# Weighting v three neighbours at a time in row groups of TensorE, with the last convolution group moved from ScalarE taps to TensorE

## The chip, the cores and the metric

The kernel runs on one core of one Trainium2 chip. The metric is the device time of one execution in microseconds (us); the median of several executions is given. A profile of one execution shows what each engine did: PE is TensorE (matmul) and PEld its weight loads, DVE is VectorE, ACT is ScalarE, POOL is GpSimd, and SP issues most of the DMAs.

## The reference

Two layers on `x` of shape (16, 56, 56, 384), float32. Each normalises its input in 32 groups of 12 channels (per image), applies an operation and adds the result to its input.

```
# layer 0: dilated attention; 3 dilations (1, 2, 3) of 128 channels each, 4 heads of 32 channels per dilation
qkv  = w_qkv @ groupnorm(x)
attn[n, k] = softmax_k( sum_d q[n, d] * k[neighbour k of n, d] * 32**-0.5 )    # 9 neighbours, zeros outside
y[n, d]    = sum_k attn[n, k] * v[neighbour k of n, d]
x = x + w_proj @ y + b_proj
# layer 1: depthwise 3x3 convolution, weights sign(w), zeros outside
x = x + conv3x3_depthwise(groupnorm(x), sign(clip(w, -1, 1)))
```

## The kernel before, in words

Channels lie on the 128 partitions, in three groups of 128 (`NG = 3`; group g has dilation g+1 in layer 0). Pixels are cut into chunks of 8 rows, 448 pixels (`PX`), 7 chunks per image and 112 in all (`N`). Three plans write each chunk's work into a table of steps: `plan_a` turns x to channel-major and takes the statistics of layer 0, `plan_b` does the attention, `plan_c` the convolution. Each chunk begins 9 steps (`STEP`) after the one before it; `plan_a` runs 9 chunks ahead of `plan_b`, `plan_c` 10 chunks behind. `at(when, order, piece)` notes a piece; the pieces are then emitted in order of step and, within a step, in the order SOFTMAX, SCORE, CONVOLVE, WEIGH, QUERY, QKV, PROJECT, STAGE_A, STAGE_C, NORM, LOADS. The Tile framework sets the final order on each in-order engine queue and inserts the waits; `in_one_go` keeps the matmuls of a burst together.

The pieces of a chunk that the change and the prediction touch:

- `project` (L357): k, v and q by float32 matmuls of 448 columns. `k_or_v` copies to persistent tiles with halo rows; two or three slots of them exist.
- `score` (L408) multiplies q by three shifted copies of k at once on VectorE (tile `t` of 3 x 448); `score_round` (L392) sums over the 32 channels of a head with a 0/1 matrix of 32 columns, four neighbours at once into the four column groups of TensorE.
- `softmax_1` (L418 to 429) turns the scores to pixel-major with `perm`, and VectorE takes the maximum and the difference; `softmax_2` divides by the sum; `softmax_3` (L443 to 446) splits each float32 weight into three bf16 terms; `turn_weights` (L451) turns them back, one group at a time (108 rows: 3 terms x 4 heads x 9 neighbours).
- `weigh` (L464, 467, 474), 27 times a chunk, three per step: one bf16 matmul copies one neighbour's 4 weights to the 32 channels of each head and adds the three terms (K = 108 rows, 128 columns out, PSUM tile `pb_a`, two banks in turn); VectorE multiplies by the shifted v into `w`; GpSimd adds `w` to `y`, 8 adds for each group.
- `out_project` (L488 to 494): projection, bias and residual, statistics of layer 1.
- Convolution of channel groups 0 and 1 (`JG = 2`): `load` brings three row-shifted copies of 32 channels onto 96 partitions (3 DMAs), `normalise` (L558) is 4 ScalarE instructions, `convolve` (L575) is 12 float32 matmuls of 32 columns in the four column groups, and VectorE adds the residual (L582).
- Convolution of group 2: `load_g` (1 DMA), `normalise_g` (L600), `taps_g` (L609: 9 ScalarE products with the tap's weight; L615: 2 GpSimd adds of three maps at once), `sum_g` (L620, 623: 3 GpSimd adds of one map).
- `turn` (L630) transposes the result to pixel-major; ScalarE copies it out of PSUM (L632); SP stores it.

`ps_mt` is a pool of four PSUM banks for all other matmul results; `ps_q` and `ps_s` have one bank each, `ps_bc` two: eight in all. A float32 matmul appears in the profile as two PE instructions.

Of the kernel before, what the change touches and what calls it, by code (L numbers as in the profile page):

```python
# [8 lines left out]
F32 = mybir.dt.float32  # L9
BF16 = mybir.dt.bfloat16  # L10
AF = mybir.ActivationFunctionType
ALU = mybir.AluOpType
# [14 lines left out]
NR = NG * HEADS * NTAP  # L27
K_SLOTS, V_SLOTS = 2, 3
# [4 lines left out]
def dilated_attention_then_binary_conv(  # L33
# [27 lines left out]

# [9 lines left out]
    JG = NG - 1  # L71
# [5 lines left out]
    ps_mt = ctx.enter_context(tc.tile_pool(name="ps_mt", bufs=4, space=PSUM))  # L77
    ps_q = ctx.enter_context(tc.tile_pool(name="ps_q", bufs=1, space=PSUM))
    ps_s = ctx.enter_context(tc.tile_pool(name="ps_s", bufs=1, space=PSUM))
    ps_bc = ctx.enter_context(tc.tile_pool(name="ps_bc", bufs=2, space=PSUM))  # L80
# [15 lines left out]
    perm = const.tile([P, NG, HEADS, NTAP], F32, name="perm")  # L96
    nc.gpsimd.memset(perm, 0.0)
    for p in range(NG * NTAP):
        g, o = divmod(p, NTAP)
        nc.gpsimd.affine_select(  # L100
            out=perm[:, g, :, o], in_=perm[:, g, :, o], compare_op=ALU.not_equal, fill=1.0,
            base=-(32 * (p % 4) + 4 * (p // 4)), pattern=[[-1, HEADS]], channel_multiplier=1,
        )
    permf = perm.rearrange("p g h o -> p (g h o)")
# [22 lines left out]
    spread = const.tile([NR, NTAP, P], BF16, name="spread")  # L127

    ktap = const.tile([P, NTAP], F32, name="ktap")

    kdiag = const.tile([K3, 3, JG * NQ, HD], F32, name="kdiag")
    with tc.tile_pool(name="setup", bufs=1) as setup:
# [31 lines left out]
        spread_f = setup.tile([NR, NTAP, P], F32, name="spread_f")  # L164
        nc.gpsimd.memset(spread_f, 0.0)
        for t in range(TERMS):
            nc.gpsimd.affine_select(
                out=spread_f.rearrange("r o (h d) -> r o h d", h=HEADS),
                in_=spread_f.rearrange("r o (h d) -> r o h d", h=HEADS),
                compare_op=ALU.not_equal, fill=1.0, base=-t * HEADS * NTAP,  # L170
                pattern=[[-1, NTAP], [-NTAP, HEADS], [0, HD]], channel_multiplier=1,
            )
        nc.vector.tensor_copy(spread, spread_f)

        def binary(dst, k_raw):

            kc = setup.tile(list(k_raw.shape), F32, tag="kc", name="kc")
            nc.vector.tensor_scalar(kc, k_raw, -1.0, 1.0, op0=ALU.max, op1=ALU.min)
            kn = setup.tile(list(k_raw.shape), F32, tag="kn", name="kn")
            nc.vector.tensor_single_scalar(dst, kc, 0.0, op=ALU.is_gt)  # L180
            nc.vector.tensor_single_scalar(kn, kc, 0.0, op=ALU.is_lt)
            nc.vector.tensor_sub(dst, dst, kn)
            nc.vector.tensor_sub(dst, dst, kc)
            nc.vector.tensor_add(dst, kc, dst)

        kp = setup.tile([K3, 3, NG * NQ], F32, name="kp")
        binary(kp.rearrange("p k s -> p (k s)"), k_in.rearrange("p k s -> p (k s)"))
        kg_in = setup.tile([P, NTAP], F32, name="kg_in")
        nc.scalar.dma_start(kg_in, w_conv.rearrange("y x c m -> c (y x m)")[JG * P : (JG + 1) * P, :])
        binary(ktap, kg_in)  # L190
# [7 lines left out]
        for kx in range(3):  # L198
            nc.vector.tensor_tensor(
                kdiag[:, kx],  # L200
                kp[:, kx, : JG * NQ].unsqueeze(2).to_broadcast([K3, JG * NQ, HD]),
                eye3.unsqueeze(1).to_broadcast([K3, JG * NQ, HD]),
                ALU.mult,
            )
# [8 lines left out]
    w_p = ctx.enter_context(tc.tile_pool(name="w_p", bufs=5))  # L213
    y_p = ctx.enter_context(tc.tile_pool(name="y_p", bufs=5))
    s_p = ctx.enter_context(tc.tile_pool(name="s_p", bufs=1))
    a_p = ctx.enter_context(tc.tile_pool(name="a_p", bufs=4))
    z_p = ctx.enter_context(tc.tile_pool(name="z_p", bufs=2))
    x1_p = ctx.enter_context(tc.tile_pool(name="x1_p", bufs=2))
    xg_p = ctx.enter_context(tc.tile_pool(name="xg_p", bufs=2))
    m_p = ctx.enter_context(tc.tile_pool(name="m_p", bufs=2))  # L220
# [15 lines left out]

    zg = []
    for s in range(2):
        t = const.tile([P, ROWS + 2, W + 2], F32, name=f"zg_{s}")
        nc.gpsimd.memset(t, 0.0)  # L240
        zg.append(t)

    def rows(ap):
        return ap.rearrange("p (r w) -> p r w", w=W)

# [96 lines left out]
    def plan_b(m, t0):  # L342
# [56 lines left out]
        def score(i):  # L399
# [5 lines left out]
            kw = kv[0][g][m % K_SLOTS][:, ky * d : ky * d + ROWS, 0:W]  # L405
            k3 = bass.AP(kw.tensor, kw.offset, [kw.ap[0], (d, 3), *kw.ap[1:]])
# [6 lines left out]
        NH = NSUB * NG * HEADS  # L413

        def softmax_1():
# [4 lines left out]
            for s in range(NSUB):  # L420
                nc.tensor.matmul(
                    pt[:SUB, s * NR : (s + 1) * NR], sT[:, s * SUB : (s + 1) * SUB], permf, start=True, stop=True
                )
            pt3 = pt[:SUB, : NSUB * NR].rearrange("p (h o) -> p h o", o=NTAP)
            mx = s_p.tile([SUB, NH], F32, tag="mx", name="mx")
            nc.vector.reduce_max(mx, pt3, axis=AX.X)
            had["e"] = e = s_p.tile([SUB, NH, NTAP], F32, tag="e", name="e")
            nc.vector.tensor_tensor(e, pt3, mx.unsqueeze(2).to_broadcast([SUB, NH, NTAP]), ALU.subtract)
            nc.scalar.activation(e, e, AF.Exp, scale=SCALE)

        def softmax_2():
            e = had["e"]
            sm = s_p.tile([SUB, NH], F32, tag="sm", name="sm")
            nc.vector.reduce_sum(sm, e, axis=AX.X)
            nc.vector.reciprocal(sm, sm)
            nc.vector.tensor_tensor(e, e, sm.unsqueeze(2).to_broadcast([SUB, NH, NTAP]), ALU.mult)
# [249 lines left out]
```

## Time and profile before

| | |
|---|---|
| median of 9 runs | 6162.89 us (6157.26 to 6166.74) |
| the profiled execution | 6163.63 us, span 6161.9 us |
| PE busy | 5705.5 us (93%) |
| DVE busy | 4377.7 us (71%) |
| POOL busy | 4392.4 us (71%) |
| ACT busy | 2646.5 us (43%) |
| mean granted TensorE clock | 0.947 |
| DMA queue q1 | 771.01 MB, 44.6% of 16 engines' span |

A line of the grouped view gives: line of the kernel, engine, operation, output and inputs, shapes, count, then busy time in us and the mean of one in ns, then the idle time of the engine just before and what ended it. In the timeline the columns are start, duration (both us), engine, line, operation, tiles, shapes and count; a bracket is idle time before it. Matmuls are pipelined, so their durations overlap: the distance between starts is what one costs TensorE.

### The profile page before, as it was taken

What the parts mean: (1) busy time and instruction counts of PE and PEld (TensorE: products, weight loads), DVE (VectorE), ACT (ScalarE), POOL (GpSimd) and SP (SyncE); (2) the same over time, 40 slices, a digit from 0 to 9 for tenths busy, and PEclk for the clock granted to TensorE, in tenths of its full rate; (3) what the DMA queues carried; (4) which work ended last, traced back from release to release, by engine and by line L of the source; (5) the groups of instructions that cost most, each with busy time, mean ns of one, the idle gap of its engine ahead of it and who ended that gap; (6) DMA issues with size and microseconds to landing.
All of it is one profiled execution on the core that took longest, in us unless ns stands there. A gap on an engine that the chain in (4) does not pass through costs nothing. (4 is left out here: it accounts for less than half of the span.)

```text
span 6161.9 us, 85206 instructions
## 1 busy us (share of the span) xinstructions
PE 5705.5 (93%) x28245; PEld 2659.6 (43%) x28245; DVE 4377.7 (71%) x6325; ACT 2646.5 (43%) x4697; POOL 4392.4 (71%) x3917
## 2 busy tenths in 40 slices
PE   5989999999999999999999999999999999999965
PEld 3434444444444444444444444444444444444421
DVE  3767777777777777777777777777777777777740
ACT  2213444444444444444444444444444444444435
POOL 1557677777778777777777778677777877777873
PEclk7999999999999999999999999999999999999975
DMA  4322444444444544445444444454444444433334
GB/s 145 94 78 87 124 131 135 137 133 128 127 130 139 135 127 130 123 129 138 141 132 127 134 131 134 131 141 132 128 130 132 138 136 127 132 111 110 113 97 116
DMA packets 629632, 777.07 MB, mean 126 GB/s; under 512 B 177091, under 2 KB 618950, under 8 KB 629190
## 3 DMA queue, kind: packets, MB, share of 16 engines
q1 hardware_dynamic: 624016, 771.01, 44.6%
q8 instruction: 223, 3.65, 0.3%
q14 instruction: 219, 1.79, 0.1%
q10 hardware_dynamic: 5174, 0.61, 0.1%
HBM read 468.47 MB, written 231.21 MB: 114 GB/s over the span
## 5 line engine op out<-in xcount | busy, mean ns | idle before, releaser
L474 POOL TENSOR_TENSOR y<-y,w 128x448 f32<-128x448 f32 x2352 | 2677.7, 1138 | 454.0 <-DVE w L467 320.5
L467 DVE TENSOR_TENSOR w<-pb_a,v 128x448 f32<-128x448 f32 x3024 | 1796.0, 617 | 684.1 <-PE pb_a L464 425.9
L357 PE MATMUL pkv<-xn,wqkvT 128*128 128x448 f32 x4032 | 1684.1, 554 | 0.0
L408 DVE TENSOR_TENSOR t<-pq,k 128x1344 f32<-128x1344 f32 x1008 | 1545.9, 1547 | 98.5 <-PE pq L357 86.4
L357 PEld LDWEIGHTS pkv<-xn,wqkvT 128*128 128x128 f32 x4032 | 779.1, 195 | 716.8 <-issue 690.1
L464 PE MATMUL pb_a<-aT,spread 108*128 108x448 bf16 x3024 | 946.6, 362 | 148.0 <-DVE w L467 138.7
L615 POOL TENSOR_TENSOR m<-m 128x1344 f32<-128x1344 f32 x224 | 680.8, 3039 | 347.0 <-ACT m L609 335.4
L357 PE MATMUL pq<-xn,wqkvT 128*128 128x448 f32 x2016 | 907.4, 562 | 0.0
L488 PE MATMUL po<-y,wprojT 128*128 128x448 f32 x2016 | 830.6, 540 | 7.7 <-POOL y L474 7.7
L392 PE MATMUL ps<-t,sel 128*32 128x448 f32 x6048 | 782.5, 570 | 41.3 <-DVE var L276 15.3
L609 ACT ACTIVATE m<-zg,ktap 128x448 f32<-128x448 f32 x1008 | 592.3, 658 | 384.7 <-POOL m L615 378.8
L575 PE MATMUL pc<-z,kdiag 96*32 96x440 f32 (+1 forms) x5376 | 577.5, 565 | 83.2 <-ACT z L558 47.8
L558 ACT ACTIVATE z<-z,mrz 96x448 f32<-96x448 f32 x896 | 626.0, 758 | 28.8 <-DMA z<-x1d 28.8
L464 PEld LDWEIGHTS <-spread 108*128 108x128 bf16 x3024 | 239.3, 98 | 804.8 <-issue 743.5
L474 POOL TENSOR_TENSOR y<-w 128x448 f32<-128x448 f32 x336 | 383.4, 1141 | 271.4 <-DVE w L467 270.2
L491 DVE SCALAR_TENSOR_TENSOR xr<-po,bias,xr 128x448 f32<-128x448 f32 x336 | 228.9, 681 | 442.7 <-PE po L488 436.8
L488 PEld LDWEIGHTS po<-y,wprojT 128*128 128x128 f32 x2016 | 382.4, 190 | 344.9 <-issue 306.7
L357 PEld LDWEIGHTS pq<-xn,wqkvT 128*128 128x128 f32 x2016 | 401.8, 200 | 268.1 <-issue 240.0
L582 DVE TENSOR_TENSOR x<-pc,x 128x448 f32<-128x448 f32 x224 | 139.8, 624 | 397.0 <-PE pc L575 396.7
L367 ACT COPY v<-pkv 128x448 f32<-128x448 f32 x336 | 177.0, 527 | 552.9 <-PE pkv L357 552.9
L329 ACT COPY xa<-pt_x 128x448 f32<-128x448 f32 x336 | 178.7, 533 | 480.7 <-PE pt_x L325 478.9
L353 ACT ACTIVATE xn<-xn,mr 128x448 f32<-128x448 f32 x336 | 233.1, 754 | 283.0 <-DMA xn<-xd 173.4
(110 smaller groups left out, 4428.9 us busy)
## 6 DMA issues: line engine op xcount, KB each, us to landing
z<-x1d SPq DMA_DIRECT2D x608, 224.0 KB, 3.9
xin<-in_x_dram SPq DMA_DIRECT2D x112, 672.0 KB, 7.5
xd<-xa SPq DMA_DIRECT2D x336, 224.0 KB, 2.2
xn<-xd SPq DMA_DIRECT2D x112, 672.0 KB, 4.5
xr<-xd SPq DMA_DIRECT2D x112, 672.0 KB, 4.1
x1d<-xr SPq DMA_DIRECT2D x112, 672.0 KB, 3.2
out_dram<-osb SPq DMA_DIRECT2D x448, 168.0 KB, 2.3
x<-x1d SPq DMA_DIRECT2D x112, 448.0 KB, 3.9
```

Source lines behind the costliest of these rows:

```text
L353: nc.scalar.activation(xj, xj, AF.Identity, bias=mr0[b][:, j, 0:1], scale=mr0[b][:, j, 1:2])
L357: nc.tensor.matmul(dst[:, :PX], wqkvT[:, cc, o0 : o0 + P], had["xn"][:, cc, :], start=(cc == 0), stop=(cc == NG - 1))
L392: return nc.tensor.matmul(had["ps"][32 * j : 32 * j + 32, :PX], sel[:, s0 : s0 + 32], tk, start=(i == 0), stop=(p + NQ >= NG * NTAP),)
L408: nc.vector.tensor_tensor(t.rearrange("p k (r w) -> p k r w", w=W), q3, k3, ALU.mult)
L464: nc.tensor.matmul(pb[:, :PX], spread[:, o, :], had[f"a{g}"], start=True, stop=True)
L467: nc.vector.tensor_tensor(rows(w), rows(pb[:, :PX]), vw, ALU.mult)
L474: nc.gpsimd.tensor_tensor(y, had["w0"] if o == 1 else y, w, ALU.add)
L488: nc.tensor.matmul(po[:, :PX], wprojT[:, g, j * P : (j + 1) * P], had[f"y{g}"], start=(g == 0), stop=(g == NG - 1))
L558: nc.scalar.activation(z[:, q], z[:, q], AF.Identity, bias=mrz[:, j, q, 0:1], scale=mrz[:, j, q, 1:2])
L575: return nc.tensor.matmul(pcr[q * HD : (q + 1) * HD, :, lo:hi], kdiag[:, kx, j * NQ + q, :], rows(z[:, q])[:, :, lo + kx - 1 : hi + kx - 1 ...
L609: nc.scalar.activation(rows(t[:, kx]), zp[:, ky : ky + ROWS, kx : kx + W], AF.Copy, scale=ktap[:, o : o + 1])
L615: nc.gpsimd.tensor_tensor(had["m"], had["m"], t, ALU.add)
```

## The change

Attention weights are ordered otherwise, so that each pair of neighbours lies in one of four 32-row blocks (24 rows used: 3 terms x 2 neighbours x 4 heads) after turning. `weigh(i)` handles three neighbours of one kernel row: three matmuls of K = 24 rows, each in another row group of TensorE, into three PSUM banks of one tile; one VectorE product of 3 x 448; GpSimd adds tiles of three, and sums the three parts at the end (per group 2 adds of 3 x 448 and 2 of 448). `turn_weights` runs four times on 128 rows in place of three times on 108, two per step. `ps_bc` has one buffer of three banks in place of two of one; `ps_mt` has three banks in place of four. The ScalarE taps of convolution group 2 are gone; that group goes through `load`, `normalise` and `convolve` like the other two.

```diff
-    ps_mt = ctx.enter_context(tc.tile_pool(name="ps_mt", bufs=4, space=PSUM))
+    ps_mt = ctx.enter_context(tc.tile_pool(name="ps_mt", bufs=3, space=PSUM))
-    ps_bc = ctx.enter_context(tc.tile_pool(name="ps_bc", bufs=2, space=PSUM))
+    ps_bc = ctx.enter_context(tc.tile_pool(name="ps_bc", bufs=1, space=PSUM))
...
-    w_p = ctx.enter_context(tc.tile_pool(name="w_p", bufs=5))
+    w_p = ctx.enter_context(tc.tile_pool(name="w_p", bufs=4))
...
-    z_p = ctx.enter_context(tc.tile_pool(name="z_p", bufs=2))
+    z_p = ctx.enter_context(tc.tile_pool(name="z_p", bufs=3))
...
+    def place(p):
+        g, o = divmod(p, NTAP)
+        return NG * o + g
...
+    def three(t, d, ky):
+        tw = t[:, ky * d : ky * d + ROWS, 0:W]
+        return bass.AP(tw.tensor, tw.offset, [tw.ap[0], (d, 3), *tw.ap[1:]])
...
-        def weigh(p):
-            g, o = divmod(p, NTAP)
-            d, (ky, kx) = DIL[g], divmod(o, 3)
-            pb = ps_bc.tile([P, 512], F32, tag="bc", name="pb_a")
-            nc.tensor.matmul(pb[:, :PX], spread[:, o, :], had[f"a{g}"], start=True, stop=True)
-            w = w_p.tile([P, PX], F32, tag="w", name="w")
-            vw = kv[1][g][m % V_SLOTS][:, ky * d : ky * d + ROWS, kx * d : kx * d + W]
-            nc.vector.tensor_tensor(rows(w), rows(pb[:, :PX]), vw, ALU.mult)
...
+        def weigh(i):
+            g, ky = divmod(i, 3)
+            pb = ps_bc.tile([P, 3, 512], F32, tag="bc", name="pb_a")
+            def copy(kx):
+                v = place(3 * i + kx)
+                lo = 32 * (v // 2 % 4)
+                rows_of = slice(lo, lo + 2 * TERMS * HEADS)
+                return nc.tensor.matmul(
+                    pb[:, kx, :PX], spread[rows_of, v % 2, :], had[f"a{v // 8}"][rows_of, :], start=True, stop=True
+                )
+            in_one_go([lambda kx=kx: copy(kx) for kx in (2, 0, 1)])
+            w = w_p.tile([P, 3, PX], F32, tag="w", name="w")
+            nc.vector.tensor_tensor(
+                w.rearrange("p k (r w) -> p k r w", w=W),
+                pb[:, :, :PX].rearrange("p k (r w) -> p k r w", w=W), three(kv[1][g][m % V_SLOTS], DIL[g], ky), ALU.mult,
+            )
+            if ky == 0:
+                had["w0"] = w
+                return
+            w0 = had["w0"]
+            nc.gpsimd.tensor_tensor(w0, w0, w, ALU.add)
+            if ky == 2:
+                had[f"y{g}"] = y = y_p.tile([P, PX], F32, tag="y", name="y")
+                nc.gpsimd.tensor_tensor(y, w0[:, 0], w0[:, 1], ALU.add)
+                nc.gpsimd.tensor_tensor(y, y, w0[:, 2], ALU.add)
...
-        for p in range(NG * NTAP):
-            at(t0 + 13 + p // 3, WEIGH, lambda p=p: weigh(p))
+        for u in range(NPAD // 8):
+            at(t0 + 12 + u // 2, SOFTMAX, lambda u=u: turn_weights(u))
+        for i in range(9):
+            at(t0 + 13 + i, WEIGH, lambda i=i: weigh(i))
...
-            nc.sync.dma_start(x1, chunk_of(x1d[b], c)[:, :JG])
+            nc.sync.dma_start(x1, chunk_of(x1d[b], c))
...
-        at(t0 - 4, LOADS, load_g)
-        at(t0 - 1, NORM, normalise_g)
-        for ky in range(3):
-            at(t0 + 2 * ky, CONVOLVE, lambda ky=ky: taps_g(ky))
-        for kx in (1, 2, 3):
-            at(t0 + 5 + kx, CONVOLVE, lambda kx=kx: sum_g(kx))
-        for j in range(JG):
+        for j in range(NG):
             at(t0 - 4 + 3 * j, LOADS, lambda j=j: load(j))
             at(t0 - 1 + 3 * j, NORM, lambda j=j: normalise(j))
             at(t0 + 2 + 3 * j, CONVOLVE, lambda j=j: convolve(j))
```

The softmax keeps its instructions, on tiles ordered neighbour-major (maximum and sum now run over a strided axis); its three-term split works on 512 elements a partition in place of 432.

## The prediction

> **What bounds the kernel now.** I read the page's engine totals first, then PE's timeline over one chunk, then the grouped instructions, the table of windows and the waits.
>
> ```profile
> PE 5705.5 (93%) x28245; PEld 2659.6 (43%) x28245; DVE 4377.7 (71%) x6325; ACT 2646.5 (43%) x4697; POOL 4392.4 (71%) x3917
> ```
>
> PE is the suspect, but busy PE is pipelined time, so the timeline has to say how full it is. PE, a stretch inside one image:
>
> ```profile
> 3006.81 0.94 PE L421 MATMUL pt_s<-perm,sT 128*112 128x108 f32 x8
> ...
> 3031.34 2.42 PE L575 MATMUL pc<-z,kdiag 96*32 96x448 f32 x24
> 3033.69 0.55 PE L464 MATMUL pb_a<-aT,spread 108*128 108x448 bf16 x2
> 3034.08 1.67 PE L357 MATMUL pq<-xn,wqkvT 128*128 128x448 f32 x4
> 3035.59 0.35 PE L464 MATMUL pb_a<-aT,spread 108*128 108x448 bf16 x1
> 3035.78 0.92 PE L357 MATMUL pq<-xn,wqkvT 128*128 128x448 f32 x2
> 3036.53 2.42 PE L488 MATMUL po<-y,wprojT 128*128 128x448 f32 x6
> 3038.88 0.96 PE L392 MATMUL ps<-t,sel 128*32 128x448 f32 x8
> 3039.77 0.55 PE L464 MATMUL pb_a<-aT,spread 108*128 108x448 bf16 x2
> 3040.16 1.67 PE L357 MATMUL pkv<-xn,wqkvT 128*128 128x448 f32 x4
> ...
> 3054.76 0.94 PE L421 MATMUL pt_s<-perm,sT 128*112 128x108 f32 x8
> ```
>
> Prices come from start to start. Four halves of float32 matmuls take 35.59 - 34.08 = 1.51 us, 0.375 each. Two weight copies take 40.16 - 39.77 = 0.39, so 0.195 each. A convolution group takes 33.69 - 31.34 = 2.35 (three rounds of two passes of 0.375 make 2.25). A score burst takes 39.77 - 38.88 = 0.89, of which two passes are 0.75. And `po` x6 takes 2.35 where 6 x 0.375 is 2.25. So work in column groups costs 0.10 us on entry from full-width work and 0.14 on leaving, whatever comes next. Four matmuls in four column groups cost one pass: groups do run at once here, in columns.
>
> The two `pt_s` bursts are the same piece of successive chunks: 47.95 us apart, with no idle bracket between. Work accounts for it: 54 halves of k, v, q 20.25; 18 of `po` 6.75; seven score bursts 6.2; two convolution groups 4.7; 27 weight copies 5.27; that leaves 4.8 for the 44 small transposes and permutations and some nine entries. Undisturbed, PE sets the pace with nothing to spare.
>
> The windows are that chunk, two disturbed places around a change of image, and the tail (columns: PE, PEld, DVE, ACT, POOL busy, clock, DMA share, GB/s):
>
> ```profile
> 3000.00:3048.00 48.00, 47.94 (x249) 22.54 (x245) 37.56 (x53) 21.43 (x40) 38.00 (x33) 1.00 0.45 130
> 3100.00:3124.00 24.00, 19.23 (x83) 8.64 (x78) 18.90 (x34) 6.59 (x11) 20.46 (x20) 0.86 0.24 77
> 3243.00:3267.00 24.00, 17.70 (x70) 6.84 (x69) 15.14 (x26) 12.26 (x20) 19.71 (x17) 0.72 0.35 69
> 6000.00:6050.00 50.00, 22.22 (x120) 7.21 (x120) 2.50 (x4) 28.73 (x49) 20.89 (x14) 0.60 0.46 121
> ```
>
> Around each image PE stands idle 4.8 + 6.3 = 11 us and loses 24 x (0.14 + 0.28) = 10 us more by a lower granted clock. Over 16 images that is some 340 us. Part of it is the statistics chain, which does not change; part is this:
>
> ```profile
> PE pb_a L464 <- DVE w L467: 138.7, 166, 4.5
> DVE w L467 <- POOL y L474: 252.4, 144, 5.5
> ```
>
> PE waits for VectorE to free a `pb_a` bank, and VectorE for GpSimd to free a `w` buffer. The costs elsewhere:
>
> ```profile
> L474 POOL TENSOR_TENSOR y<-y,w 128x448 f32<-128x448 f32 x2352 | 2677.7, 1138 | 454.0 <-DVE w L467 320.5
> L467 DVE TENSOR_TENSOR w<-pb_a,v 128x448 f32<-128x448 f32 x3024 | 1796.0, 617 | 684.1 <-PE pb_a L464 425.9
> L408 DVE TENSOR_TENSOR t<-pq,k 128x1344 f32<-128x1344 f32 x1008 | 1545.9, 1547 | 98.5 <-PE pq L357 86.4
> L615 POOL TENSOR_TENSOR m<-m 128x1344 f32<-128x1344 f32 x224 | 680.8, 3039 | 347.0 <-ACT m L609 335.4
> ```
>
> **The change on the path (PE).** Per chunk, removed: 27 x 0.195 = 5.27 us.
>
> Added: nine triples in row groups. The trace has no row-group work. Upper bound: the three run one after another and pay both switches, 3 x 0.195 + 0.10 + 0.14 = 0.82. Lower bound: one pass, no switch, 0.195. The nearest row is the score pass, where four column groups share one: one bf16 pass and the 0.14 on leaving, 0.33. I take 0.33, nine times 2.97, and 0.1 for entry on three triples that do not follow a score burst (most copies follow one now), 0.3: 3.3 in all, a gain of 2.0. Bounds for the nine: 1.76 to 7.4.
>
> The Trainium skill speaks against the change here: "TensorEngine Tiling (Array Packing)", Key Properties, says that changing the tiling mode, not just the tile, drains TensorE. The 0.10 and 0.14 above agree with it for column groups; no row shows it for row groups. The page "TensorE: Matmul & The Clock Gate", Part 3, gives 3.07 times for four row tiles of K = 32 and 512 columns; by that efficiency a triple would be an estimated 0.25 us before any switch, and the gain some 1.5 us in place of 2.0.
>
> The third convolution group adds 2.35 us, or 2.45 when it does not follow a score burst: 2.4. The fourth `turn_weights` adds four transposes (3030.24 less 3029.86, three in 0.38 with a switch of tiles, is 0.1 at most each): 0.2. The permutation's 128 columns in place of 108 add about 0.1 on eight instructions.
>
> So in an undisturbed chunk PE gets 2.4 + 0.3 - 2.0 = 0.7 us longer, between -0.85 and +4.9. The copies and small parts count for 112 chunks, -190 us; the convolution for the 102 chunks that are not in the tail, +245. Sum +55 us. The change does not lighten the bound engine; it shifts load off the others onto it.
>
> **Off the path.** POOL per chunk: 24 adds of 1.14 (27.3) become 6 x 3.04 + 6 x 1.14 = 25.1; the tap adds, 2 x 3.04 + 3 x 1.14 = 9.5, vanish; the wider split adds 0.4. From 39 us (4392/112) to 28. DVE: 27 x 0.594 (1796/3024) = 16.0 becomes 9 x 1.547 = 13.9 (price of `t`, the same shape with one operand in PSUM), and 0.62 for the third residual add: 39.1 to 37.6. ACT: 9 taps of 0.66 (L609's mean, busy overlaps) and a zg of 0.85 go, 4 x 0.76 of z and one `aT` of 0.54 come: 3.2 us less. SP: three z loads come, one goes; each issue holds the queue 0.4 us in 48, with the halo copies and stores behind it, so 0.8 us, hidden; the queue idles between issues. DMA: 672 + 224 - 287 KB more per chunk, 68 MB, from 45% to 49%: hidden by landing times of 3.9 us against a lead of three steps (some 16 us). All this costs nothing while PE is full; it matters at the image changes and in the tail.
>
> At an image change, GpSimd's backlog holds `w` buffers. With 11 us less per chunk and room for nine to twelve maps instead of five, most of VectorE's 252 us of waiting should go. For PE I take back half of the 139 us of direct wait and a third of the 160 us of lost clock: -120 us. Bounds: -300 (all of both) and +60.
>
> Why +60: one `pb_a` tile of three banks now, so a triple waits until the last product (1.55 us) has ended; queued behind it on PE are that step's projections. Triples are a step (5.3 us) apart and DVE is 78% busy (37.56 of 48), so mostly it is free in time, but not during the softmax. And `ps_mt` has three banks, so a late copy on ACT holds up the projection behind. I take +20.
>
> Tail: the last image's seven convolution chunks run alone, 21 us each, with 29 of 50 us on ACT and PE at clock 0.6. Per chunk 6.8 us of ACT's taps and 9.5 of POOL's adds leave the chain, a convolution of 4 to 4.6 us at that clock enters: -20, bounds -45 and +20.
>
> Sum, against the profiled execution's 6163.6: +55 - 120 + 20 - 20 = -65, so 6099. That execution is 0.7 above the median; I say 6100.
>
> **Rivals.**
> 1. *Row groups do not run at once, or their weight loads show (slower).* One mechanism: the price of a triple on PE. Each 0.1 us on it is 9 x 112 x 0.1 = 101 us, so the forecast's gain is gone at 0.40 instead of 0.33. With two loads of 0.098 us (L464's in PEld) exposed it is 0.53, giving 6100 + 200 = 6300; run one after another at 0.82, 6100 + 490 = 6590. For it: no row of this kernel shows row groups. Against it: column groups start 7 ns apart and share a pass. Chance 0.24.
> 2. *The single `pb_a` tile becomes the wait.* If the triple stands 0.25 us on average behind VectorE's 1.55, 1008 x 0.25 = 250 us come in place of the 20: 6330. For it: softmax steps crowd DVE. Against it: three copies a step through two banks wait hardly at all now outside image changes. Chance 0.15.
> 3. *The image changes heal fully and switches are cheap.* All 300 us return and a triple costs 0.25: 6164 + 55 - 80 - 300 + 20 - 20, some 5840; half way, 5950. Against it: the statistics chain of small VectorE operations remains. Chance 0.10.
> 4. *It cancels.* PE's +55 and 20 against a recovery of 75: 6163. Chance 0.07.
>
> **How the numbers follow.** The forecast, 6100, has 0.44, with its own range 6020 to 6150. About 0.2%, 12 us, is what a measurement of this kernel can tell from no change. Faster: 0.44 and 0.10, 0.54. Same: 0.07. Slower: 0.24 and 0.15, 0.39. The range for 8 in 10 reaches from the half-way case of rival 3, 5950, to both rivals above, 6330; outside are a full recovery and row groups that run one after another.
>
> **What would show it.** In PE's timeline, `pb_a` x3 with starts some 7 ns apart and the next start about 0.33 us after the first: right; 0.5 or more, rival 1. An undisturbed chunk of 48.5 to 49 us between `pt_s` bursts. Three `pc` bursts a chunk at 2.35. POOL near 3100 us, DVE near 4200. The wait of DVE w for POOL y near nothing. PE pb_a waiting for DVE w under 100 us in all: right; over 300, rival 2. Tail chunks under 21 us. Undisturbed chunks below 47.95 would prove my sum on PE wrong.

## The result, and the profile after

The changed kernel takes 6187.59 us, the median of 9 runs (6184.60 to 6199.42), against 6163.20 us for the kernel before in 29 runs: a ratio of 1.0043 with a 95% interval of 1.0035 to 1.0051. It is slower by 0.4%, where 6100 and a gain were forecast. It lies outside the forecast's own range (6020 to 6150), but inside the wide one (5950 to 6330), whose upper end had been set by two rivals that did not come true.

The profiled execution's span grew from 6161.9 to 6189.3 us. The engine totals after:

```profile
PE 5774.6 (93%) x31381; PEld 2601.6 (42%) x31381; DVE 4312.8 (70%) x4415; ACT 2344.6 (38%) x4137; POOL 3162.7 (51%) x2066
```

GpSimd and ScalarE are relieved as forecast (POOL from 4392.4 us, ACT from 2646.5); PE has more to do than before, also as forecast (from 5705.5 us). The TensorE timeline over one chunk inside an image, between two `pt_s` bursts as before:

```profile
3001.88 1.04 PE L429 MATMUL pt_s<-perm,sT 128*112 128x128 f32 x8
...
3033.14 0.96 PE L394 MATMUL ps<-t,sel 128*32 128x448 f32 x8
3034.03 0.36 PE L472 MATMUL pb_a<-aT,spread 24*128 24x448 bf16 x3
3034.33 4.78 PE L359 MATMUL pkv<-xn,wqkvT 128*128 128x448 f32 x12
3038.94 2.42 PE L504 MATMUL po<-y,wprojT 128*128 128x448 f32 x6
...
3050.70 1.04 PE L429 MATMUL pt_s<-perm,sT 128*112 128x128 f32 x8
```

The chunk takes 3050.70 - 3001.88 = 48.82 us, 47.95 before; 48.65 was forecast. Three copies and the switch after them take 3034.33 - 3034.03 = 0.30 us: the row groups run at once. But twelve projection halves behind them take 4.61 us (3038.94 - 3034.33) where twelve at 0.375 and nothing else make 4.50. The excess lies in the first of them, which takes 0.480 us to the next start where the others take 0.376. So this triple costs some 0.40 us, not 0.33.

The windows view, first over one chunk, then over 4000 us that hold many changes of image (columns as before: PE, PEld, DVE, ACT, POOL busy, clock, DMA share, GB/s). After:

```profile
3000.00:3048.00 48.00, 47.87 (x270) 21.57 (x268) 36.08 (x34) 20.06 (x36) 27.41 (x14) 1.00 0.55 157
1000.00:5000.00 4000.00, 3812.12 (x21041) 1729.82 (x21042) 2887.56 (x2956) 1566.13 (x2770) 2107.90 (x1311) 0.96 0.49 141
```

Before:

```profile
1000.00:5000.00 4000.00, 3826.21 (x19192) 1793.36 (x19191) 2980.19 (x4297) 1792.54 (x3186) 2980.62 (x2609) 0.97 0.47 132
```

Inside an image PE is full in both. Over the long window it stood idle for 188 us after and 174 before, and the granted clock was 0.96 and 0.97. POOL has lost 870 us of work in that window and PE stands idle for longer. So the losses around the changes of image, which the forecast saw shrink, did not. The waits show what holds TensorE now. After:

```profile
PE ps L394 <- DVE var L284: 109.0, 30, 6.3
PE pb_a L472 <- DVE w L478: 84.3, 36, 4.2
```

Before, the score burst waited for the statistics at other links, and shortly. One of them:

```profile
PE ps L392 <- DVE var L278: 12.6, 13, 1.1
```

All idle time just before these bursts was 41.3 us before and is 172.1 us after. Lines 264 to 296 of the changed kernel are the statistics of one image: about a dozen small VectorE operations, with TensorE in between, one after another. They run twice for each image (layer 0 and layer 1). The score burst does not need them; L284 is only the last thing before it in the queue. The TensorE timeline at one such place, after:

```profile
2370.26 0.96 PE L394 MATMUL ps<-t,sel 128*32 128x448 f32 x8 [1.10 <-DVE var L280]
2377.54 1.72 PE L394 MATMUL ps<-t,sel 128*32 128x448 f32 x8 [6.32 <-DVE var L284]
2379.19 1.44 PE L294 MATMUL pp<-pair,gselT 32*128 32x2 f32 x6
...
2382.78 3.60 PE L590 MATMUL pc<-z,kdiag 96*32 96x448 f32 x24
2386.31 0.60 PE L327 MATMUL pt_x<-ident,xin 112*128 112x112 f32 x4
```

VectorE at the same time:

```profile
2370.13 0.14 DVE L280 RECIPROCAL var<-var 32x1 f32<-32x1 f32 x1
2370.20 1.53 DVE L478 TENSOR_TENSOR w<-pb_a,v 128x1344 f32<-128x1344 f32 x1
2371.65 0.27 DVE L282 TENSOR_TENSOR var<-var 32x1 f32<-32x1 f32 x1
2371.85 1.54 DVE L409 TENSOR_TENSOR t<-pq,k 128x1344 f32<-128x1344 f32 x1
2373.32 2.70 DVE L283 TENSOR_TENSOR var<-var 32x1 f32<-32x1 f32 x1
2375.95 1.54 DVE L409 TENSOR_TENSOR t<-pq,k 128x1344 f32<-128x1344 f32 x1
2377.41 0.13 DVE L284 TENSOR_SCALAR var<-var 32x1 f32<-32x1 f32 x1
```

And GpSimd:

```profile
2372.97 3.03 POOL L486 TENSOR_TENSOR w<-w 128x1344 f32<-128x1344 f32 x1
```

Between each link of the chain and the next stands, here, a product of three maps, 1.53 or 1.54 us: one of the weighing (L478) and two of the scores (L409, the same before the change). A product of one number for each of 32 partitions (L283) takes 2.70 us: it ends at 2376.02, and GpSimd's three-map add ends at 2376.00. The second `t` product starts only then, and the score burst waits for it. TensorE stands for 6.32 us, and then runs slower: the score burst takes 1.65 us to the next start where 0.89 is usual, the convolution group 3.53 us where 2.35 is. The granted clock is 1.00 from 2355 to 2370 us, 0.60 from there to 2377.5, and 0.69 to 2390.

For the comparisons below, each profile gives three numbers: the undisturbed chunk; the time from one image to the next, 7 chunks, as a mean over the images in the middle; and the difference, which is what one image loses at its change:

| kernel | chunk, us | image, us | lost per image, us | both chains, us |
|---|---|---|---|---|
| before | 47.96 | 366.6 | 30.9 | 28.1 |
| after | 48.80 | 372.0 | 30.4 | 35.0 |

The last column is the time from the first VectorE operation behind a matmul of the chain (L264) to the last one on `pair` (L286), the two layers added. The loss of an image is not one stop. In the kernel before it is spread over most of the seven chunks (by their place in the image, their medians are 48.8, 57.7, 51.8, 62.9, 48.1, 49.1 and 48.0 us); in the changed kernel two chunks carry it (63.2 and 66.6), and one of 46.9 gives a little back. TensorE stands idle for 15.6 us of an image before and 17.1 after; most of the rest goes with a lower granted clock in the same chunks (0.89 in the longest of them before, 0.87 after).

The difference of 27.4 us in span lies so: first 14 chunks -29.5 (ten of them have no convolution beside them), twelve images in the middle +65.3, the last 13 chunks +5.1, the tail after the last `pt_s` -12.6, the head -1.0.

### The profile page after: what moved, and what is told of

The parts are those of the page before. It is cut to its first block, busy times and chain, and to the rows that moved or that the text cites. A ratio compares the mean times of both kernels' runs of the same rounds, so it can differ in the third digit from the quotient of the medians.

```text
span 6189.3 us, 84655 instructions
## 1 busy us (share of the span) xinstructions
PE 5774.6 (93%) x31381; PEld 2601.6 (42%) x31381; DVE 4312.8 (70%) x4415; ACT 2344.6 (38%) x4137; POOL 3162.7 (51%) x2066
## 5 line engine op out<-in xcount | busy, mean ns | idle before, releaser
L486 POOL TENSOR_TENSOR w<-w 128x1344 f32<-128x1344 f32 x672 | 2045.9, 3045 | 1504.3 <-DVE w L478 1372.4
L478 DVE TENSOR_TENSOR w<-pb_a,v 128x1344 f32<-128x1344 f32 x1008 | 1556.9, 1545 | 296.3 <-PE pb_a L472 290.7
L409 DVE TENSOR_TENSOR t<-pq,k 128x1344 f32<-128x1344 f32 x1008 | 1543.4, 1549 | 216.3 <-PE pq L359 214.5
L590 PE MATMUL pc<-z,kdiag 96*32 96x440 f32 (+1 forms) x8064 | 941.3, 570 | 55.0 <-ACT z L573 32.1
L573 ACT ACTIVATE z<-z,mrz 96x448 f32<-96x448 f32 x1344 | 938.2, 758 | 142.9 <-DMA z<-x1d 126.7
L394 PE MATMUL ps<-t,sel 128*32 128x448 f32 x6048 | 781.5, 570 | 172.1 <-DVE var L284 109.0
L597 DVE TENSOR_TENSOR x<-pc,x 128x448 f32<-128x448 f32 x336 | 209.9, 625 | 615.0 <-PE pc L590 615.0
L590 PEld LDWEIGHTS pc<-z,kdiag 96*32 96x32 f32 x8064 | 273.4, 115 | 586.0 <-issue 499.2
L472 PE MATMUL pb_a<-aT,spread 24*128 24x448 bf16 x3024 | 378.9, 364 | 97.0 <-DVE w L478 84.3
L452 POOL TENSOR_TENSOR rest<-ew,e 112x512 f32<-112x512 f32 x112 | 129.9, 1160 | 596.3 <-ACT e L451 524.8
L490 POOL TENSOR_TENSOR y<-y,w 128x448 f32<-128x448 f32 x336 | 382.8, 1139 | 26.3
L489 POOL TENSOR_TENSOR y<-w 128x448 f32<-128x448 f32 x336 | 382.0, 1137 | 22.5
L472 PEld LDWEIGHTS <-spread 24*128 24x128 bf16 x3024 | 105.1, 91 | 600.2 <-issue 568.3
## 6 DMA issues: line engine op xcount, KB each, us to landing
xin<-in_x_dram SPq DMA_DIRECT2D x112, 672.0 KB, 5.5
xn<-xd SPq DMA_DIRECT2D x112, 672.0 KB, 4.7
xr<-xd SPq DMA_DIRECT2D x112, 672.0 KB, 4.3
x1d<-xr SPq DMA_DIRECT2D x112, 672.0 KB, 3.1
x<-x1d SPq DMA_DIRECT2D x112, 672.0 KB, 4.7
```

The source lines that it names most:

```text
L394: return nc.tensor.matmul(had["ps"][32 * j : 32 * j + 32, :PX], sel[:, s0 : s0 + 32], tk, start=(i == 0), stop=(p + NQ >= NG * NTAP),)
L409: nc.vector.tensor_tensor(t.rearrange("p k (r w) -> p k r w", w=W), q3, k3, ALU.mult)
L472: return nc.tensor.matmul(pb[:, kx, :PX], spread[rows_of, v % 2, :], had[f"a{v // 8}"][rows_of, :], start=True, stop=True)
L478: nc.vector.tensor_tensor(w.rearrange("p k (r w) -> p k r w", w=W), pb[:, :, :PX].rearrange("p k (r w) -> p k r w", w=W), three(kv[1][g][m ...
L486: nc.gpsimd.tensor_tensor(w0, w0, w, ALU.add)
L489: nc.gpsimd.tensor_tensor(y, w0[:, 0], w0[:, 1], ALU.add)
```

## Experiments

### The two halves alone

The change is two changes in one: the packing of the copies, and the convolution of group 2 moved to TensorE. The first kernel is the changed one with the convolution of before (and one buffer fewer in three pools, to make room for its tiles); the second is the kernel before with the convolution of the changed one.

```diff
 first: changed kernel, with load_g, normalise_g, taps_g and sum_g of before
+        for ky in range(3):
+            at(t0 + 2 * ky, CONVOLVE, lambda ky=ky: taps_g(ky))
-        for j in range(NG):
+        for j in range(JG):
-    xa_p bufs=3; y_p bufs=5; a_p bufs=6; z_p bufs=3
+    xa_p bufs=2; y_p bufs=4; a_p bufs=5; z_p bufs=2
 second: kernel before, without them
-        for j in range(JG):
+        for j in range(NG):
-    z_p bufs=2
+    z_p bufs=3
```

> The row-group weighing alone; channel group 2 of the convolution stays on ScalarE and GpSimd. (For space, aT has five buffers, y four and xa two, in place of six, five and three.) Theory: a triple costs TensorE 0.29 us as in the trace of the changed kernel, so nine cost 2.6 where 27 copies cost 5.27; less 0.3 for the fourth turning, an undisturbed chunk falls from 47.95 to 45.6 us, and the time to 6163 - 112 x 2.35 = 5900. The loss at the image changes stays near 30 us per image. Rival: GpSimd (28 + 9.5 = 37.5 us of work per chunk) and VectorE (37 us) now fill 82% of such a chunk and set new waits on TensorE: 5980 to 6060, with TensorE idle inside the images.

> The third convolution group on TensorE alone; the weighing as before, with four ps_mt banks and two pb_a banks. Theory: 2.4 us of TensorE per chunk in 102 chunks, undisturbed chunk 50.3, time 6163 + 245 = 6408, a little less for the tail: 6390. Rival: the 9.5 us per chunk that GpSimd loses free the w buffers and heal half of the image changes (240 us of 480): 6160 to 6290.

Packing only: 6034.33 us, ratio 0.9772 (0.9755 to 0.9788). Convolution only: 6152.81 us, ratio 0.9967 (0.9956 to 0.9978).

| kernel | chunk, us | image, us | lost per image, us | both chains, us |
|---|---|---|---|---|
| packing only | 46.60 | 358.6 | 32.4 | 36.3 |
| convolution only | 50.20 | 367.4 | 16.0 | 22.5 |

Each half alone is faster than the kernel before beside which it was run, and the two together slower. In the undisturbed chunk they add: -1.36 and +2.24 make +0.88, and +0.84 was seen. At the changes of image they do not. The moved convolution brings the loss from 30.9 to 16.0 us; with the packing on top it is back at 30.4. The windows say the same. Packing only:

```profile
1000.00:5000.00 4000.00, 3790.51 (x19932) 1735.91 (x19924) 2966.10 (x2992) 1876.99 (x3338) 2894.88 (x1726) 0.95 0.48 135
```

Convolution only:

```profile
1000.00:5000.00 4000.00, 3937.21 (x21015) 1832.22 (x21013) 3006.15 (x4369) 1536.32 (x2731) 2276.85 (x2245) 0.98 0.52 144
```

PE idles for 209 us in the first and 63 in the second. In the first the score burst waits for the statistics at the same link and as long as in the changed kernel; in the second, as in the kernel before, at another link and shortly. Packing only:

```profile
PE ps L411 <- DVE var L301: 113.0, 30, 6.3
```

Convolution only:

```profile
PE ps L387 <- DVE var L273: 13.7, 14, 1.1
```

So this wait comes with the packing. The convolution alone heals the image changes as the forecast had named it, with GpSimd's and ScalarE's work for the taps gone: 15 us less per image, more than the 5.6 us by which the chains got shorter. Which part of the taps' work made the rest was not taken apart. The expectation that the convolution alone would cost its full price in every chunk, 6390, missed for that reason; the rival's 6160 to 6290 was nearer and still too high. The packing alone was expected at 5900 with a chunk of 45.6 us; the chunk is 46.60, because a triple costs more than the 0.29 us taken, and that makes most of the miss. The rival's range, 5980 to 6060, holds the 6034, but not for its reason: TensorE is idle for 0.15 us of such a chunk, so no new wait stands inside the images.

### Is it GpSimd's long instruction?

The packing brings two things to VectorE: products of three maps, and GpSimd adds of three maps beside it. The first experiment cuts the add.

```diff
-            nc.gpsimd.tensor_tensor(w0, w0, w, ALU.add)
+            for kx in range(3):
+                nc.gpsimd.tensor_tensor(w0[:, kx], w0[:, kx], w[:, kx], ALU.add)
```

> The changed kernel, with each GpSimd add of three maps (3.05 us) split into three adds of one map (1.14 us). Theory: at an image change the small VectorE operations of the statistics (two SBUF inputs; 1.34 us mean at L283, up to 2.7) stand until GpSimd's running instruction ends, so shorter instructions shorten the chain: the six such operations fall from 144 us in all to about 100, the time from 6187 to 6145 to 6170. Rival: the loss at the image changes is VectorE's in-order queue of 1.55 us products and the single pb_a tile; GpSimd's instruction length does not matter: 6180 to 6195, or a little more for 2.3 us more GpSimd work per chunk.

Measured: 6187.88 us, ratio 1.0021 (1.0011 to 1.0031). The median is the changed kernel's, but in the rounds of this run the kernel before took 6175.51 us in place of 6163.20; by the ratios, 1.0021 against 1.0043, some 0.2% or 13 us may have gone. The loss is 30.4 us per image, unchanged, and the chains are 34.1. The six small operations of two inputs (L271, L272, L282, L283, L285, L286) went from 144 to 109 us in the whole run. The length of GpSimd's instruction is not what brought back the 14 us per image (230 us in all).

The second keeps GpSimd and gives these six operations another form, in which the second operand is one scalar for each partition:

```diff
-        nc.vector.tensor_mul(dev, dev, dev)
-        nc.vector.tensor_add(dev, dev, ch[:, :, 1])
+        for j in range(NG):
+            nc.vector.tensor_scalar(dev[:, j : j + 1], dev[:, j : j + 1], dev[:, j : j + 1],
+                                    ch[:, j, 1:2], op0=ALU.mult, op1=ALU.add)
-        nc.vector.tensor_mul(t, r, r)
-        nc.vector.tensor_mul(t, t, v)
+        nc.vector.tensor_scalar(t, r, r, v, op0=ALU.mult, op1=ALU.mult)
 ... and both operations on pair
```

> The changed kernel, with the statistics' small VectorE operations written with per-partition scalar operands, so that none reads two SBUF tensors (three multiply-adds in place of two for dev, one in place of two for var, tensor_scalar for both of pair). Theory: each takes 0.13 to 0.15 us as the scalar ones do now; the 144 us in all fall to about 30, and the time falls by 60 to 130 us, to 6060 to 6130. Rival: the chain's length is its crossings between TensorE, VectorE and ScalarE behind 1.55 us products, not these waits: within 15 us of 6187.

Measured: 6121.82 us, ratio 0.9916 (0.9901 to 0.9932), inside the theory's 6060 to 6130: 66 us less than the changed kernel by the medians, 1.3% by the ratios (the rounds are those of the run above). The groups by shape, changed kernel:

```profile
L283 DVE TENSOR_TENSOR var<-var 32x1 f32<-32x1 f32 x32 | 42.8, 1338 | 0.1
```

The scalar form, both places:

```profile
L272 DVE TENSOR_SCALAR dev<-dev,ch 128x1 f32<-128x1 f32 x96 | 18.6, 245 | 0.1
L284 DVE TENSOR_SCALAR var<-var 32x1 f32<-32x1 f32 x32 | 8.1, 253 | 0.1
```

The operations take 39 us in the whole run instead of 144, the chains 30.1 instead of 35.0, and the loss per image is 26.2. This is a part, 4 of the 14 us that the packing had brought back. It is not the hold by GpSimd alone: the new form also makes one link out of two, in `dev` and in `var`. The Trainium skill, "SBUF — State Buffer", section "Who interferes with whom", states that a VectorE instruction with two SBUF inputs contends with a GpSimd instruction that reads SBUF, and that one with at most one SBUF input, outside VectorE's two-port modes, does not. The 2.70 us of L283 and the 0.25 us of the scalar form, of which none took over 0.28, agree with it.

### Is it the length of the product?

```diff
-            nc.vector.tensor_tensor(
-                w.rearrange("p k (r w) -> p k r w", w=W),
-                pb[:, :, :PX].rearrange("p k (r w) -> p k r w", w=W), three(kv[1][g][m % V_SLOTS], DIL[g], ky), ALU.mult,
-            )
+            for kx in (2, 0, 1):
+                vw = kv[1][g][m % V_SLOTS][:, ky * d : ky * d + ROWS, kx * d : kx * d + W]
+                nc.vector.tensor_tensor(rows(w[:, kx]), rows(pb[:, kx, :PX]), vw, ALU.mult)
```

This leaves the copies, the single `pb_a` tile and GpSimd as they are in the changed kernel.

> The changed kernel with VectorE's product of three maps (1.55 us) as three products of one map (0.6 us), into the same tiles. If the length of the product on VectorE's in-order queue, behind which the statistics' small operations and the score products stand, makes the 14 us: the loss per image falls from 30 to about 20 and the time to 6020 to 6080, since 2.1 us more of VectorE per chunk are hidden (38 of 48.8 us). If it is the single tile of three banks or the missing bank: 6180 to 6230.

Measured: 5995.63 us, ratio 0.9731 (0.9711 to 0.9751), 192 us faster than the changed kernel and better than expected. The undisturbed chunk is 48.98 us, 0.18 longer; the loss per image falls to 16.0 us, the value of the convolution alone; the chains to 19.5. VectorE's timeline at a change of image, three products:

```profile
2427.76 0.62 DVE L481 TENSOR_TENSOR w<-pb_a,v 128x448 f32<-128x448 f32 x1
2428.29 0.15 DVE L271 TENSOR_TENSOR dev<-dev 128x3 f32<-128x3 f32 x1
2428.36 0.62 DVE L481 TENSOR_TENSOR w<-pb_a,v 128x448 f32<-128x448 f32 x1
2428.89 0.15 DVE L272 TENSOR_TENSOR dev<-dev,ch 128x3 f32<-128x3 f32 x1
```

The same two links in the changed kernel:

```profile
2503.81 1.22 DVE L271 TENSOR_TENSOR dev<-dev 128x3 f32<-128x3 f32 x1
2504.96 1.54 DVE L478 TENSOR_TENSOR w<-pb_a,v 128x1344 f32<-128x1344 f32 x1
2506.42 1.04 DVE L272 TENSOR_TENSOR dev<-dev,ch 128x3 f32<-128x3 f32 x1
```

A link of the chain waits behind 0.6 us in the one, behind 1.5 us in the other. These two links are also not held by a GpSimd add here (0.15 us each, against 1.22 and 1.04), but others still are: the six small operations take 102 us in the whole run, against 144. The window:

```profile
1000.00:5000.00 4000.00, 3911.84 (x21815) 1769.03 (x21814) 3063.06 (x4460) 1617.01 (x2874) 2211.45 (x1361) 0.98 0.52 147
```

PE idles for 88 us in it instead of 188, with VectorE doing more instructions for the same work (4460 against 2956). Cutting the one product into three takes back the whole of what the packing had cost at the changes of image, with the row groups, their tile and GpSimd's adds in place. So the length of the product is what brings the loss back.

The same cut of the other long product, that of the scores:

```diff
-            nc.vector.tensor_tensor(t.rearrange("p k (r w) -> p k r w", w=W), q3, k3, ALU.mult)
+            for kx in range(3):
+                nc.vector.tensor_tensor(rows(t[:, kx]), qg, kw, ALU.mult)
```

> The changed kernel with the score's product (tile t, 1.55 us) as three products of one map, and the weighing's product left whole. If it is the length of the pieces on VectorE's in-order queue that stretches the statistics chain, it should not matter which of the two products is cut: chain from pair to pair from 17 to 18 us down to 10 to 13, loss per image from 30 to about 20, time 6020 to 6090. If only the weighing's own product matters (because pb_a is freed sooner): 6180 to 6210.

Measured: 6119.83 us, ratio 0.9932 (0.9917 to 0.9946). The loss per image falls as expected, to 18.6 us (chains 26.5), though this product is as long in the kernel before: it is the pieces between the links that count, whichever they are. But the undisturbed chunk grows to 49.57 us, 0.75 more, and 112 of those eat 84 us; so the time of 6020 to 6090 was missed. TensorE is idle for 0.54 us of such a chunk instead of 0.14. Why the scores' cut costs a full pipeline so much more than the other was not followed further.

### Is it the single tile of three banks?

Two runs for the term of +20 in the forecast. The kernel before with three banks in `ps_mt`:

```diff
-    ps_mt = ctx.enter_context(tc.tile_pool(name="ps_mt", bufs=4, space=PSUM))
+    ps_mt = ctx.enter_context(tc.tile_pool(name="ps_mt", bufs=3, space=PSUM))
```

> The kernel before, with three ps_mt banks in place of four; nothing else. Does the bank that the row-group tile takes explain why the packing costs 14 us per image at the image changes (loss per image: 16 us with the convolution alone moved, 30 us with the packing too)? If the bank does: 6163 + 16 x 14 = 6390, with undisturbed chunks still 48 us. If the granularity of the product or the single pb_a tile does: 6150 to 6180.

Measured: 6160.61 us, ratio 0.9994 (0.9982 to 1.0006). In the kernel before, the fourth bank is worth nothing.

And the three products, each with a `pb_a` tile of its own, so that a bank comes free after one product and not after three:

```diff
-    ps_bc = ctx.enter_context(tc.tile_pool(name="ps_bc", bufs=1, space=PSUM))
+    ps_bc = ctx.enter_context(tc.tile_pool(name="ps_bc", bufs=3, space=PSUM))
...
-            pb = ps_bc.tile([P, 3, 512], F32, tag="bc", name="pb_a")
+            pb = {kx: ps_bc.tile([P, 512], F32, tag="bc", name="pb_a") for kx in (2, 0, 1)}
```

> As the kernel with three products, and pb_a as three tiles of one bank each, so that the first matmul of the next triple waits for the first product alone. If TensorE's wait for the whole tile makes the loss: 60 to 150 us below the kernel with three products. If not: within 15 us of it.

Measured: 6059.75 us, ratio 0.9834 (0.9816 to 0.9851): 64 us slower than the three products with one tile, which neither alternative had foreseen. The loss per image is 19.0 in place of 16.0 and the chains 23.1 in place of 19.5, with TensorE idle as long (7.9 us of an image in both); the first 14 chunks and the tail take 18 and 14 us more. Separate tiles do not help; why they hurt is open.

### Is it the chain?

If a chain of short links loses time because each link stands behind long work in one step of the schedule, it should lose less where each link has a step of its own. The statistics are cut into five pieces, one per step, with all else unchanged:

```diff
-            at(t0 + 5, STAGE_A, norm)
+            for n, piece in enumerate(stats_pieces(...)):   # aggregate, mean, deviation, variance, finish
+                at(t0 + 5 + n, STAGE_A, piece)
-            at(t0 + 27, PROJECT, norm)
+            for n, piece in enumerate(stats_pieces(...)):
+                at(t0 + 27 + n, PROJECT, piece)
```

In the changed kernel:

> The changed kernel with the statistics chain of each image cut into five pieces, one step (5.4 us) apart each; nothing is needed before 8 steps later. Theory: the loss at an image change is TensorE standing, in its order, at the chain's matmuls and at the score bursts whose products stand behind the chain on VectorE, and the lower clock that follows; with a step between crossings nothing waits: loss per image from 30 to 5 or 10 us, time 6187 - 16 x 22 = 5830. Rival: the loss comes from GpSimd's halo memsets and the slots of k and v at the image change, not from the statistics: 6170 to 6200.

In the kernel before:

> The kernel before, with its statistics chain spread over five steps. If half of its 31 us of loss per image is the chain and half GpSimd's backlog (31 us before against 16 us with the convolution moved): the chain's half goes, 6163 - 16 x 12 = 5970, with 10 to 18 us per image left. If the backlog makes nearly all of it: 6100 to 6160.

Changed kernel: 5950.09 us, ratio 0.9655 (0.9637 to 0.9673). Kernel before: 5905.05 us, ratio 0.9579 (0.9559 to 0.9599). The loss per image goes from 30.4 to 14.6 and from 30.9 to 11.6. So 16 and 19 us of each image's loss hang on where the chain stands, in both kernels: more than half. For the kernel before this is more than the half that was expected; for the changed kernel it is less, by 120 us. What is left there shows in the timelines of the changed kernel with spread statistics. VectorE:

```profile
2431.03 2.69 DVE L298 TENSOR_TENSOR var<-var 32x1 f32<-32x1 f32 x1
```

GpSimd beside it:

```profile
2430.67 3.04 POOL L502 TENSOR_TENSOR w<-w 128x1344 f32<-128x1344 f32 x1 [1.16 <-DVE var L296]
```

TensorE, the second score burst after it:

```profile
2437.70 1.72 PE L410 MATMUL ps<-t,sel 128*32 128x448 f32 x8 [1.50 <-DVE var L300]
```

The variance piece still has several links in one step, and the first of them is held until GpSimd's add ends (2430.67 + 3.04 = 2433.71, and 2431.03 + 2.69 = 2433.72). One chunk in each image takes 59 us there.

### The parts put together

Packing only, with spread statistics and the scalar form; and the same with three products:

```diff
 packing only
+ five pieces of the statistics, one per step
+ tensor_scalar in place of tensor_mul / tensor_add on dev, var and pair
 second kernel: also
+            for kx in (2, 0, 1): product of one map
```

> The row-group weighing with group 2 left on ScalarE and GpSimd, statistics spread over five steps and with scalar operands. Undisturbed chunks of 46.6 us; loss per image from 32 to 5 or 12 us: 6034 - 16 x 24 = 5650, between 5600 and 5760. If GpSimd's backlog (37.5 us of work in 46.6) takes the place of the chain: 5800 to 5900.

> The same with three products of one map. If the chain is gone from the path, shorter products bring nothing more, and 2.1 us more of VectorE per chunk (39 of 46.6) may cost: 5640 to 5700. If the products' length still delays something: 20 to 60 us below the kernel with one product.

Measured: 5633.02 us, ratio 0.9142 (0.9126 to 0.9158), and 5661.04 us, ratio 0.9186 (0.9171 to 0.9200). The first was expected at 5650. The window of the first:

```profile
1000.00:5000.00 4000.00, 3985.62 (x21563) 1826.46 (x21560) 3122.62 (x3228) 2030.38 (x3618) 3139.90 (x1868) 1.00 0.50 146
```

PE idles for 14 us of 4000 and the granted clock is 1.00. The loss per image is 5.5 us and the chunk 46.60. The saving over the kernel before, 530 us, is near what the two numbers give: (30.9 - 5.5) x 16 = 406 for the images and 1.36 x 112 = 152 for the chunks, 558. With the chain off the path the cut of the product brings nothing any more; it costs 28 us. This version beats both kernels: it keeps the packing, leaves the convolution of group 2 on ScalarE, and moves nothing onto TensorE, which has no room. The changed kernel, with the convolution moved, was not run with both repairs.

## Why the prediction was wrong

By its terms, with 16 images and 112 chunks:

| term | predicted, us | measured, us | from |
|---|---|---|---|
| copies and small parts in row groups | -190 | -152 | 1.36 x 112, packing only |
| third convolution group | +245 | +228 | 2.24 x 102, convolution only |
| changes of image | -120 | -8 | 0.5 x 16 |
| single tile, three banks | +20 | 0 | the run with three banks; `pb_a` waits for VectorE 84.3 us, 138.7 before |
| tail | -20 | -13 | section after the last `pt_s` |
| sum | -65 | +55 | |

The sum of the measured terms is 28 us above the span's +27.4; the first 14 chunks gained 19 us more than these terms give them, and that is most of it. It is the packing's: the first 14 chunks take 702.8 us before, 672.0 with the packing only and 698.7 with the convolution only. In the sixth to eighth chunk of the kernel before, TensorE waits 4.0 us a chunk at `pa` for GpSimd's last split of the weights, and a chunk takes 49.4 us; in the changed kernel the wait is 0.6 us and the chunk takes 44.5.

**The step that failed is the term of -120 for the changes of image.** The forecast read 21 us of loss for an image from two windows; the chunks show 30.9. The mechanism that it named was there, and stronger than taken: without GpSimd's and ScalarE's work for the taps an image loses 15 us less, 240 us in all, twice what was taken back. VectorE's wait for GpSimd's buffers, 252.4 us before, is nearly gone. The group of its products, changed kernel, by shape, has 2.6 and 1.8 us of it at the end:

```profile
L478 DVE TENSOR_TENSOR w<-pb_a,v 128x1344 f32<-128x1344 f32 x1008 | 1556.9, 1545 | 296.3 <-PE pb_a L472 290.7 <-POOL w L486 2.6 <-POOL y L489 1.8
```

But the forecast wrote "Part of it is the statistics chain, which does not change". It does: the two chains grew from 28.1 to 35.0 us, and from 22.5 to 35.0 against the kernel that has the moved convolution alone. The forecast counted the product of three maps only as work, 13.9 us a chunk in place of 16.0, a relief for an engine off the path. It did not ask what stands behind such a product in VectorE's queue. There a link of the chain waits up to 1.54 us behind a product of the weighing instead of 0.6. It can then be held by a GpSimd add of 3.04 us, of which a chunk has six; the kernel before has two, in the taps, beside 24 of 1.14. This gave back 14.4 us per image, 230 in all. The upper bound of +60 for this term was set for the single `pb_a` tile, which is not the cause; the -8 lies between the bounds for a reason that neither was drawn for.

Nor are the chain and GpSimd's backlog two separate parts, as the forecast split them. In the kernel before, moving the taps away takes 15 of the 31 us, and spreading the chain with the taps in place takes 19, together more than there is. So some of the loss goes with either; how the two hang together was not taken apart.

**Right.** The chunk between `pt_s` bursts, 48.82 against 48.65, and so the statement that the change shifts load onto the engine that bounds the kernel. Three copies at once: the third starts 7 ns after the first. So rival 1 is wrong in its mechanism, and its price was nearly reached: by the chunk of the packing alone a triple costs (5.27 - 1.36 - 0.3 - 0.3) / 9 = 0.37 us in the mean, if the two terms of 0.3 hold, above the 0.33 taken and below the 0.40 at which the gain was to be gone. In the trace the next start comes 0.294 us after the first copy. Where a projection follows, its first half takes 0.10 us more, 0.40 together; where a score burst follows, nothing is added. Three `pc` bursts a chunk. POOL near 3100 (3162.7). The wait of `w` for `y` near nothing. PE waiting for VectorE in `pb_a` under 100 us (84.3): rival 2 fails.

**Missed besides.** DVE near 4200 was 4312.8, of which the held small operations are 30 us more than before (144.1 against 114.3) and the softmax's sum, now over a strided axis, 36 (102.6 against 66.5). The fourth bank cost nothing. The tail's -13 is near the -20, but not by its mechanism: the last convolution chunks were to take under 21 us each and take 22 to 24 in the middle of the tail, from one chunk's last copy out of PSUM to the next (20.5 to 22 before). The last eight of these distances make 169.0 us, against 166.9 before; the gain lies ahead of them, behind the last `pt_s`.

**Not foreseen by any rival.** None of the four named the chain growing longer. Rival 4, that the terms cancel at 6163, is nearest in its number, and for its own reason is wrong too: the recovery was not small, it was undone. The word of rival 3 against a full recovery, that the chain remains, was the thing to follow further.

**Open.** The exact shares of the place in VectorE's queue and of the hold by GpSimd. Cutting the add left the loss as it was, the scalar form gave 4 us, cutting the product gave all. With the product cut, the small operations are still held for 102 of 144 us in the whole run, 42 us or 2.6 per image less, while the chains are 15.5 us per image shorter; so the place in the queue makes the larger part. Why separate tiles are slower.

## What to carry to other kernels

When small instructions are merged into long ones on an in-order engine, look for a chain of short dependent operations in the same queue: each link then waits for a longer neighbour, and the price lies on the chain's path though the engine's total fell. Give each link of such a chain a step of its own in the schedule (6163 to 5905 here with nothing else changed), and try the scalar-operand form for tiny operations beside a busy GpSimd (1.3% in the changed kernel). And when two edits come as one change, price and run each alone: here one was worth 2.3%, the other 0.3%, and together they cost 0.4%.

## What the runs showed of the hardware that was not expected

- A VectorE operation with two tensor inputs of 32 x 1 can be held until the GpSimd add beside it ends: 2.70 and 2.69 us, to within 0.02 us of the add's end, where the shortest of the same line took 0.14. The form with a scalar operand took 0.25 us in the mean.
- Three row-group copies start 3 to 4 ns apart and cost 0.294 us to the next start. The first float32 half behind them takes 0.480 us instead of 0.376; behind a full-height copy, in the kernel before, it took 0.380.
- After 6.32 us of waiting TensorE ran slower for the next bursts, at a granted clock of 0.69: a score burst of 1.65 us instead of 0.89 and a convolution group of 3.53 instead of 2.35. With PE idle 14 us of 4000 the granted clock was 1.00; with 209 us idle, 0.95. So a wait costs TensorE more than its length.
